# Attention prologue: the first pair's 1/std row on ScalarE's queue, z's projection one step behind its transposes, its exps one group behind, and group norm's power ahead of z's

## The chip, the cores and the metric

The kernel runs on one core of one Trainium2 chip. A core has five engines that run their own instruction streams in order: TensorE (PE, with its weight loads shown apart as PEld), VectorE (DVE), ScalarE (ACT), GpSimd (POOL) and SyncE (SP, which here only starts DMA transfers). The metric is the device time in microseconds (us) of one execution. The kernel before took 3403.12 us (median of three runs, 3402.76 to 3403.5).

## The reference

Two attention layers, each added to its input x of 128 rows x 256 positions x 256 channels, in float32. The change touches only what comes ahead of layer 0.

```python
# layer 0
x = x + attention0(_gn(x), z)              # group norm over 32 groups, no weights
# in attention0, m = _gn(x):
m_norm = layer_norm(m, ln_m_w, ln_m_b)     # per position: needs 1/std of each position
z_norm = layer_norm(z, ln_z_w, ln_z_b)     # z: 256 x 256 x 128
q, k, v = (m_norm @ W.T for W in (Wq, Wk, Wv))   # 8 heads of 32
b = (z_norm @ Wb.T).transpose(...)         # one bias per head, query and key
p = softmax(q @ k.T * scale + b)
o = (p @ v) * sigmoid(m @ Wg.T + bg)
# layer 1
x = x + banded_attention(_gn(x))           # 4 heads of 64, band of 16
```

So before layer 0 can begin, two things are wanted of all of x and all of z: the mean and 1/std of each group of channels of x, and exp(b), a table of 8 x 256 x 256 numbers that every row of the layer multiplies its exponentials by.

## The kernel before

The work has three stages: the prologue, layer 0's loop over 64 pairs of rows, and layer 1's loop over 64 pairs. The order within the prologue and the loops is written out by hand: each engine executes its instructions in the order in which the program emits them, and a tile framework adds the waits.

**z.** The 256 x 256 positions of z come in 16 jobs of 2 MB. `z_front` (L1057) loads a job into one of three buffers `zt`, takes its statistics on DVE (16 `bn_stats`, L1069), and has GpSimd raise the variance to the power -1/2 (`zrs`, L1078). `z_back` (L1081) is called one job later. It works in two steps for each job, four for each group of two jobs: 16 transposes on PE into four PSUM tiles `ps_t` (L1092; three buffers), four copies by ScalarE into `zT` (L1094; ten buffers), and four matmuls on four column tiles of 32 that project onto the 8 heads, into `ps_b` (L1097; eight PE instructions, two passes for each float32 matmul). After the fourth step, ScalarE copies `ps_b` to `bT` (L1104), PE turns it back (`ps_k`, L1107), DVE multiplies by 1/std (`bt`, L1113) and ScalarE takes eight exps into the table `eb` (L1118).

**x.** Between the jobs, eight blocks of x (4 MB each, `x_block`, L1123) are loaded and their group statistics taken on DVE (L1127). After the last, in the body of job 8, `x_moments` (L1129) and `moments_steps` (L961) merge them: a matmul for the mean (L966), one for the variance (L975), a power on GpSimd (`rs_l`, L979), and copies that spread the result over channels (L984).

**The first pair.** The function `starts` (L1404) is a generator that is advanced twice for each job, in the middle of z's statistics and at the end of the body. In turn it runs the moments, loads of pairs 0 to 2 of x, `centre` and `scale` (group norm on GpSimd, L1175 and L1178), `moments` and `root` (1/std of each position, L1188 to L1199), `fetch` (L1204), `turn` (transposes, L1215, then the multiplication by the row on GpSimd, L1221), and the first projections of q and k (L1234, L1238). `root` ends with a DMA that writes the 512 values of 1/std to DRAM (`rs_d`, four-byte pieces, 2 KB); `fetch` reads them back as a row broadcast to all 128 partitions (`rs_r`, 256 KB). Both stand in SyncE's queue, which is also that of all loads of z and x. When job 15 is through, pair 1 is centred, scaled and measured, and layer 0's loop begins with `now.scores(0, 0)` (L1268).

Of the kernel before, what the change touches and what calls it, by code (L numbers as in the profile page):

```python
# [9 lines left out]
F32 = mybir.dt.float32  # L10
AF = mybir.ActivationFunctionType
# [5 lines left out]
P = 128  # L17
# [4 lines left out]
def bcast(ap, axis, n):  # L22

    ap = ap.unsqueeze(axis)
    shape = list(ap.shape)
    shape[axis] = n
    return ap.broadcast_to(shape)
# [746 lines left out]
def fast_kernel(  # L774
# [25 lines left out]
    nc = tc.nc  # L800
    S, I, C = x.shape
    CZ = z.shape[2]
    H = wbT.shape[1]
# [4 lines left out]
    NB = I // P  # L808
    KC = C // P
    NP = S // 2  # L810
    N2 = 2 * I
# [97 lines left out]
    eb = const.tile([P, H, NB, I], F32, name="eb")  # L909
# [9 lines left out]
    for a in range(KC):  # L919
        for h in range(H1):  # L920
            n = P // H1
# [11 lines left out]
    for h in range(H1):  # L933
        n = P // H1
# [9 lines left out]
    bz_r = const.tile([P, H], F32, name="bz_r")  # L944
# [45 lines left out]
    pps = tc.alloc_tile_pool(name="pre_ps", bufs=2, space=PSUM)  # L990

    def mm(name):
        return ps_mm.tile([P, 512], F32, name=name, tag="mm")
# [5 lines left out]
    for w, dst in ((wq, qb), (wk, kb)):  # L999
        for m in range(KC):  # L1000
            ps = mm("b_ps")
            for k in range(KC):
                nc.tensor.matmul(
                    ps[:, 0:1], w[:, k, m * P : (m + 1) * P], lnb_c[:, k : k + 1],
                    start=(k == 0), stop=(k == KC - 1),
# [36 lines left out]
    nga = S // GA  # L1042
# [6 lines left out]
    IB, IS = 32, 64  # L1049
    zjobs = [(b, i) for b in range(NB) for i in range(0, I, IB)]  # L1050
    z_rows = z.rearrange("(u t) (p b) c -> t p u (b c)", t=NB, b=NB)
    wbz = pz.tile([P, 4, 4, H], F32, name="wbz")
# [4 lines left out]
    def z_front(b, i0):  # L1057

        nonlocal zrs
        zt = pz.tile([P, IB, CZ], F32, name="zt", tag="zt", bufs=3)  # L1060
        nc.sync.dma_start(
            zt.rearrange("p (u b) c -> p u (b c)", b=NB), z_rows[b, :, i0 // NB : (i0 + IB) // NB, :]
        )

        st = pz.tile([P, IB, 3], F32, name="zst", tag="zst", bufs=2)
        for i in range(0, IB, 2):
            if i == IB // 2:
                step()
            nc.vector.bn_stats(  # L1069
                st[:, i : i + 2, :].rearrange("p i f -> p (i f)"),  # L1070
                zt[:, i : i + 2, :].rearrange("p i c -> p c i"),
            )
        at = i0 % IS
        if at == 0:
            zrs = pz.tile([P, IS], F32, name="zrs", tag="zrs", bufs=3)
        rs = zrs[:, at : at + IB]
        nc.vector.tensor_scalar(rs, st[:, :, 2], 1.0 / CZ, 1e-5, ALU.mult, ALU.add)
        nc.gpsimd.tensor_tensor(rs, rs, mhalf[:, :IB], ALU.pow)  # L1078
        return zt, zrs

    def z_back(b, i0, zt, rs):  # L1081
        nonlocal ps_b
        at = i0 % IS
        if at == 0:
            ps_b = pps.tile([P, 512], F32, name="ps_b", tag="bias", bufs=1)
        for j in range(at // 16, (at + IB) // 16):
            zTs = []
            for g in range(4):
                ps_t = pps.tile([P, 512], F32, name="ps_t", tag="zT", bufs=3)
                i = (4 * j + g) * 4 - at  # L1090
                for a in range(4):
                    nc.tensor.transpose(ps_t[:, a * P : (a + 1) * P], zt[:, i + a, :], ident)  # L1092
                zT = pz.tile([P, 512], F32, name="zT", tag="zT", bufs=10)
                nc.scalar.copy(zT, ps_t)  # L1094
                zTs.append(zT)
            for g in range(4):
                nc.tensor.matmul(  # L1097
                    ps_b[32 * g : 32 * (g + 1), :], wbz[:, j].rearrange("p a h -> p (a h)"), zTs[g],
                    start=(j == 0), stop=(j == 3),
                )  # L1100
        if at + IB < IS:
            return
        bT = pz.tile([P, 512], F32, name="bT", tag="bT", bufs=2)
        nc.scalar.copy(bT, ps_b)  # L1104
        ps_k = pps.tile([P, 4, 4, 4, H], F32, name="ps_k", tag="keys", bufs=1)
        for a in range(4):
            nc.tensor.transpose(  # L1107
                ps_k[:, a].rearrange("p g j h -> p (g j h)"), bT[:, a * P : (a + 1) * P], ident
            )
        bt = pz.tile([P, IS, H], F32, name="bt", tag="bt", bufs=2)  # L1110
        for j in range(4):
            q = slice(j * 16, (j + 1) * 16)
            nc.vector.tensor_tensor(  # L1113
                bt[:, q, :].rearrange("p (g a) h -> p g a h", g=4), ps_k[:, :, :, j, :].rearrange("p a g h -> p g a h"),
                bcast(rs[:, q].rearrange("p (g a) -> p g a", g=4), 3, H), ALU.mult,
            )
        for h in range(H):
            nc.scalar.activation(  # L1118
                eb[:, h, :, b * P + (i0 - at) // NB : b * P + (i0 - at + IS) // NB],
                bt[:, :, h].rearrange("p (u b) -> p b u", b=NB), AF.Exp, bias=bz_r[:, h : h + 1],  # L1120
            )

    def x_block(j):  # L1123
        xa = px.tile([P, GA * NB, C], F32, name="xa", tag="xa", bufs=2)
# [24 lines left out]
    NT = 2 * NB  # L1149
    x1 = [dram.tile([GB, I, C], F32, name=f"x1_{j}") for j in range(S // GB)]  # L1150
    rs_d = [dram.tile([NT * P], F32, name=f"rs_d{p}") for p in range(NP)]
# [8 lines left out]
    class Pair:  # L1160
# [35 lines left out]
        def root(self):  # L1196

            nc.gpsimd.tensor_tensor(self.rs, self.rs, mhalf[:, :NT], ALU.pow)
            nc.sync.dma_start(rs_d[self.p].rearrange("(t p) -> p t", p=P), self.rs)  # L1199

        def fetch(self):

            self.rs_r = la.tile([P, NT * P], F32, name="rs_r", tag="rs_r", bufs=2)
            nc.sync.dma_start(self.rs_r, rs_d[self.p].unsqueeze(0).broadcast_to([P, NT * P]))  # L1204


        def turn(self, pss=None):
            self.xgT = la.tile([P, KC, N2], F32, name="xgT", tag="xgT", bufs=2)
            self.xnT = la.tile([P, KC, N2], F32, name="xnT", tag="xnT", bufs=2)
            if pss is None:  # L1210
                ps = ps_s.tile([P, KC, N2], F32, name="ps_x", tag="s")
                pss = [ps[:, k, :] for k in range(KC)]
            for k in range(KC):
                for t in range(NT):
                    nc.tensor.transpose(  # L1215
                        pss[k][:, t * P : (t + 1) * P], self.xg[:, t, k * P : (k + 1) * P], ident
                    )
            for k in range(KC):
                nc.scalar.copy(self.xgT[:, k, :], pss[k])
            for k in range(KC):  # L1220
                nc.gpsimd.tensor_tensor(self.xnT[:, k, :], self.xgT[:, k, :], self.rs_r, ALU.mult)  # L1221

# [175 lines left out]
    def pair(p):  # L1398
        return Pair(p) if p < NP else Nobody()

    zrs = ps_b = la = lb = ps_s = ps_o = M0 = R0 = None
    now = nxt = nn = None

    def starts():  # L1404

        nonlocal la, M0, R0, now, nxt, nn
        steps = x_moments()
        next(steps)
        yield
        next(steps)  # L1410
        yield
        next(steps)
        px.release()
        la = tc.alloc_tile_pool(name="l0_early", bufs=1, side="left", reuse_waits="tile")
        now = pair(0)
        yield
        M0, R0 = next(steps)
        now.centre()
        now.scale()
        yield  # L1420
        nxt = pair(1)
        yield
        now.moments(0)
        now.moments(1)
        now.root()
        yield
        nn = pair(2)
        yield
        yield
        now.fetch()  # L1430
        yield
        now.turn([mm("ps_x") for _ in range(KC)])
        yield
        yield
        now.project("qT", 0)
        now.project("kT", 0)
        yield

    start = iter(())

    def step():
        next(start, None)


    behind, nx = None, 0
    with tc.manual_schedule():
        for n, job in enumerate(zjobs):
            front = z_front(*job)
            if behind is not None:
                z_back(*behind)  # L1450
            behind = (*job, *front)
            if nx < nga and nx * 9 <= n * nga:
                x_block(nx)
                nx += 1
                if nx == nga:
                    start = starts()
            step()
        assert nx == nga
        z_back(*behind)
        for _ in start:  # L1460
            pass
        for f in ("centre", "scale"):
            getattr(nxt, f)()
        for r in range(2):
            nxt.moments(r)
# [8 lines left out]
    with tc.manual_schedule():  # L1474
        old = was = Nobody()
        es = nn3 = None
        for p in range(NP):

            nxt.root()
            ps = now.scores(0, 0)  # L1480
            e = now.add_bias(0, 0, ps)
            was.apply(1, 1, es)
# [30 lines left out]
            now.project("gT", 1)  # L1513
            now.gate(0, 1)
            nxt.turn()
            was.normalize(0)
            now.values(1)
            now.keep_values(1)
# [16 lines left out]
            old, was, now, nxt, nn = was, now, nxt, nn, nn3  # L1535
# [39 lines left out]
    with tc.tile_pool(name="l1", bufs=2) as sb, tc.tile_pool(  # L1575
        name="l1s", bufs=4
    ) as sm, tc.tile_pool(name="ps1_mm", bufs=2, space=PSUM) as ps_mm, tc.tile_pool(
        name="ps1_s", bufs=1, space=PSUM
# [160 lines left out]
        def pair1(p):  # L1739
            return Pair1(p) if p < NP else Nobody()  # L1740
# [15 lines left out]
        now, nxt = pair1(0), pair1(1)  # L1756
# [15 lines left out]
        with tc.manual_schedule():  # L1772
            was = Nobody()
            for p in range(NP - 1):
                nn = pair1(p + 2)
# [23 lines left out]
                was, now, nxt = now, nxt, nn  # L1799
# [87 lines left out]
```

## Time and profile before

| | busy us | share of the span |
|---|---|---|
| PE | 3253.1 | 96% |
| PEld | 2041.4 | 60% |
| DVE | 2027.8 | 60% |
| ACT | 1463.2 | 43% |
| POOL | 1974.5 | 58% |

The profile's span is 3403.3 us. Shares over the whole span say little of the prologue, which ends at 269.64 us with the first scores, 8% of the span. These groups of instructions, taken from the stretch 0 to 270 us, are its work:

| line, engine, what | count | busy us | mean ns |
|---|---|---|---|
| L1069 DVE bn_stats of z | 256 | 86.5 | 416 |
| L1127 DVE bn_stats of x | 128 | 77.2 | 684 |
| L1078 POOL power of z's variances | 16 | 86.8 | 5430 |
| L1092 PE transposes of z | 512 | 75.7 | 305 |
| L1097 PE projection of z | 256 | 66.1 | 691 |
| L1094 ACT copies of the transposes | 128 | 66.9 | 594 |
| L1118 ACT exps | 56 | 17.1 | 387 |

A PE time of one instruction includes its pipeline, so overlapping instructions add up to more than the stretch they fill; start-to-start distances are the better measure there.

### The profile page before, as it was taken

To read this page: it belongs to the slowest core of one execution; us is meant where nothing else is said; L and a number is where in the kernel's file an instruction comes from. 1 tells how busy PE (TensorE), PEld (TensorE's weight loads), DVE (VectorE), ACT (ScalarE), POOL (GpSimd) and SP (SyncE) were. 2 spreads that over 40 slices of the span, in tenths; PEclk is the share of its full clock that TensorE was granted. 3 is DMA by queue.
4 is the path that set the end of the run, shared out by engine and by line. 5 is a ranking of instruction groups with operands and counts; after the bars stand their busy time and mean duration, and the time that the engine had idled before them with its cause. 6 is when DMAs were issued, how large, how long until landed. Compare 5 with 4: busy or idle time off the path is not lost. (4 is left out here: it accounts for less than half of the span.)

```text
span 3403.3 us, 81181 instructions
## 1 busy us (share of the span) xinstructions
PE 3253.1 (96%) x35158; PEld 2041.4 (60%) x35158; DVE 2027.8 (60%) x3218; ACT 1463.2 (43%) x2121; POOL 1974.5 (58%) x1377
## 2 busy tenths in 40 slices
PE   5479999999999999999999999799999999999998
PEld 3245555555555555555555555577676777767676
DVE  6955566676666666666666665366544444344455
ACT  2244444444444444444444443344444444444443
POOL 2357778877777777877787775233333333333332
PEclk8789999999999999999999999899999999999999
DMA  9941122222221222222122211212111121211211
GB/s 333 376 133 27 47 73 73 73 48 73 73 73 48 73 73 60 61 73 72 42 69 68 73 48 57 77 52 64 52 57 59 52 64 52 62 54 52 64 57 53
DMA packets 198815, 262.91 MB, mean 77 GB/s; under 512 B 46288, under 2 KB 147536, under 8 KB 197296
## 3 DMA queue, kind: packets, MB, share of 16 engines
q1 hardware_dynamic: 198448, 257.61, 24.9%
q8 instruction: 279, 4.57, 0.7%
q14 instruction: 88, 0.72, 0.1%
HBM read 188.82 MB, written 68.75 MB: 76 GB/s over the span
## 5 line engine op out<-in xcount | busy, mean ns | idle before, releaser
L1289 POOL TENSOR_TENSOR eboth<-e 128x512 f32<-128x512 f32 x512 | 640.5, 1273 | 379.2 <-DVE e L1284 361.7
L1284 DVE TENSOR_TENSOR e<-ps_sc,eb 128x1024 f32<-128x1024 f32 x512 | 603.0, 1219 | 316.1 <-ACT ps_sc L1275 226.5
L1275 ACT ACTIVATE ps_sc<-ps_sc 128x1024 f32<-128x1024 f32 x512 | 492.7, 1006 | 506.6 <-PE ps_sc L1268 506.6
L1676 POOL TENSOR_TENSOR e<-e,bw 128x384 f32<-128x384 f32 x256 | 259.9, 1038 | 443.3 <-ACT e L1674 443.3
L1637 PE MATMUL ps_p<-xgT,w_in 128*128 128x512 f32 x1024 | 468.4, 600 | 0.1
L1629 POOL TENSOR_TENSOR xt<-xt,bout_r 128x1024 f32<-128x1024 f32 x64 | 152.4, 2381 | 382.7 <-PE ps_x L1626 382.7
L1729 DVE TENSOR_TENSOR yo<-ps_y,xt 128x512 f32<-128x512 f32 x128 | 88.4, 690 | 379.6 <-PE ps_y L1725 379.6
L1637 PEld LDWEIGHTS ps_p<-xgT,w_in 128*128 128x128 f32 x1024 | 188.6, 190 | 199.1 <-issue 166.0
L1268 PE MATMUL ps_sc<-qT,kT 32*128 32x256 f32 x4096 | 293.7, 400 | 0.8 <-ACT kT L1238 0.8
L1299 PE MATMUL ps_ov<-e,v 128*32 128x256 f32 x4096 | 274.1, 385 | 0.5 <-DVE oT L1313 0.5
L1234 PE MATMUL ps_p<-xnT,wq 128*128 128x512 f32 x512 | 254.2, 618 | 0.7 <-POOL xnT L1221 0.6
L1234 PE MATMUL ps_p<-xgT,wg 128*128 128x512 f32 x512 | 253.9, 618 | 0.0
L1725 PE MATMUL ps_y<-w_out,oT 128*128 128x256 f32 x1024 | 249.8, 387 | 2.6 <-DVE oT L1710 2.6
L1341 PE MATMUL ps_y<-wo,oT 128*128 128x256 f32 x1024 | 244.8, 382 | 7.1 <-POOL oT L1331 7.1
L1341 PEld LDWEIGHTS ps_y<-wo,oT 128*128 128x128 f32 x1024 | 196.3, 192 | 88.4 <-issue 59.7
L1249 PE MATMUL ps_v<-wv,xnT 128*128 128x256 f32 x1024 | 242.2, 379 | 1.3 <-ACT qT L1238 1.3
L1268 PEld LDWEIGHTS ps_sc<-qT,kT 32*128 32x128 f32 x4096 | 185.4, 184 | 92.5 <-issue 70.7
L1234 PE MATMUL ps_p<-xnT,wk 128*128 128x512 f32 x512 | 240.6, 592 | 0.0
L1652 PE MATMUL ps_v<-w_in,xgT 128*128 128x256 f32 x1024 | 231.8, 379 | 0.0
L1707 DVE RECIPROCAL rv<-odd 128x256 f32<-128x256 f32 x128 | 224.4, 1753 | 4.4
L1652 PEld LDWEIGHTS ps_v<-w_in,xgT 128*128 128x128 f32 x1024 | 194.4, 190 | 53.5 <-issue 30.1
L1249 PEld LDWEIGHTS ps_v<-wv,xnT 128*128 128x128 f32 x1024 | 189.6, 190 | 52.5 <-issue 30.6
(163 smaller groups left out, 5019.8 us busy)
## 6 DMA issues: line engine op xcount, KB each, us to landing
zt<-in_z_dram SPq DMA_DIRECT2D x16, 2048.0 KB
xa<-in_x_dram SPq DMA_DIRECT2D x8, 4096.0 KB
xt<-in_x_dram SPq DMA_DIRECT2D x64, 512.0 KB
rvb<-rsum SPq DMA_DIRECT2D x256, 128.0 KB
x<-xo SPq DMA_DIRECT2D x16, 2048.0 KB
xt<-x SPq DMA_DIRECT2D x64, 512.0 KB
out_dram<-yo SPq DMA_DIRECT2D x63, 512.0 KB
rs_r<-rs_d SPq DMA_DIRECT2D x64, 256.0 KB
```

The source lines that it names most:

```text
L1234: nc.tensor.matmul(ps, w[:, k, m * P : (m + 1) * P], getattr(self, src)[:, k, :], start=(k == 0), stop=(k == KC - 1),)
L1249: nc.tensor.matmul(self.ps_v[:, b * C : (b + 1) * C], self.xnT[:, k, t * P : (t + 1) * P], wv[:, k, :], start=(k == 0), stop=(k == KC - 1),)
L1268: nc.tensor.matmul(self.pss[q // 2][:, q % 2, b, :], self.kT[rs, c, r * I + b * P : r * I + (b + 1) * P], self.qT[rs, c, r * I : (r + 1) * I],
L1275: nc.scalar.activation(self.pss[a], self.pss[a], AF.Exp)
L1284: nc.vector.tensor_tensor(e, pss[a], eb[:, h : h + 2], ALU.mult)
L1289: nc.gpsimd.tensor_tensor(t, es[a][:, :, 0, :], es[a][:, :, 1, :], ALU.add)
L1299: nc.tensor.matmul(ov[q * D0 : (q + 1) * D0, :], self.v[:, r, b, h * D0 : (h + 1) * D0], es[q // 2][:, q % 2, b, :], start=(b == 0), stop= ...
L1341: nc.tensor.matmul(self.ps_y[:, b * C : (b + 1) * C], self.oT[r][:, k, b * P : (b + 1) * P], wo[:, k, :], start=(k == 0), stop=(k == KC - 1),)
L1637: nc.tensor.matmul(ps, w_in[:, k, n * C + m * P : n * C + (m + 1) * P], self.xgT[:, k, :], start=(k == 0), stop=(k == KC - 1),)
L1652: nc.tensor.matmul(ps[:, b * C : (b + 1) * C], self.xgT[:, k, t * P : (t + 1) * P], w_in[:, k, 2 * C : 3 * C], start=(k == 0), stop=(k == ...
L1676: nc.gpsimd.tensor_tensor(e[:, q], e[:, q], bcast(bw.rearrange("p b w -> p (b w)"), 1, KC), ALU.mult)
L1725: nc.tensor.matmul(ps[:, b * C : (b + 1) * C], self.oT[r][:, k, b * P : (b + 1) * P], w_out[:, k, :], start=(k == 0), stop=(k == KC - 1),)
```

## The change

Four edits, all in the prologue.

1. **The 1/std row through ScalarE's queue.** The DMA that was the last line of `root` becomes a method `send`, and both `send` and `fetch` take the queue as an argument. For pair 0 it is ScalarE's: `send` in the statistics of job 13, `fetch` in those of job 15. All other pairs keep SyncE's. SyncE's queue is then left to the loads of z and x.
2. **z's projection one step behind.** `z_back` emits a step's transposes and copies, then the projection of the step before (`z_project`), so that PE needn't stand and wait for the copies of what it has just transposed.
3. **Exps one group behind.** The exps of a group (`z_exp`) are emitted with the third step of the next group, so that ScalarE doesn't stop its copies for `bt`.
4. **Group norm's steps by a plan.** The generator gives way to a table `plan` of (jobs since the last block of x, quarter of a job). The second moments matmul comes after a quarter of job 9's statistics instead of a half, and `rs_l`'s power after three quarters, which puts it ahead of z's power for that job on GpSimd. The transposes of pair 0 move to the end of job 14, the multiplication by the row (`normal`, split off `turn`) to the end of job 15, and the first projections of q and k behind the last exps.

```diff
     def z_back(b, i0, zt, rs):
...
+            z_project()
+            turned = (b, i0 - at, rs, j, zTs)
+
+    def z_project():
+        nonlocal turned, ps_b
+        if turned is None:
+            return
+        (b, i0, rs, j, zTs), turned = turned, None
+        if j == 0:
+            ps_b = pps.tile([P, 512], F32, name="ps_b", tag="bias", bufs=1)
+        for g in range(4):
+            nc.tensor.matmul(
+                ps_b[32 * g : 32 * (g + 1), :], wbz[:, j].rearrange("p a h -> p (a h)"), zTs[g],
+                start=(j == 0), stop=(j == 3),
+            )
+        if j == 1:
+            z_exp()
+        if j < 3:
+            return
         bT = pz.tile([P, 512], F32, name="bT", tag="bT", bufs=2)
...
+        weighed.append((b, i0, bt))
...
-            nc.sync.dma_start(rs_d[self.p].rearrange("(t p) -> p t", p=P), self.rs)
-
-        def fetch(self):
+
+        def send(self, queue=nc.sync):
+            queue.dma_start(rs_d[self.p].rearrange("(t p) -> p t", p=P), self.rs)
+
+        def fetch(self, queue=nc.sync):
...
+    plan = {
+        (0, 4): begin, (1, 1): lambda: next(steps), (1, 3): lambda: next(steps), (1, 4): take, (2, 3): norm,
+        (3, 4): weigh,
+        (5, 3): lambda: now.send(nc.scalar),
+        (6, 4): lambda: now.turn([mm("ps_x") for _ in range(KC)]),
+        (7, 2): lambda: now.fetch(nc.scalar),
+        (7, 4): lambda: now.normal(),
+    }
...
         z_back(*behind)
-        for _ in start:
-            pass
+        z_project()
+        z_exp()
+        now.project("qT", 0)
+        now.project("kT", 0)
```

In the plan, `begin` starts the merge of x's moments, `take` loads pair 0, `norm` spreads the group norm's result, centres and scales pair 0 and loads pair 1, and `weigh` takes pair 0's moments with their power and loads pair 2. In layer 0's loop `nxt.root()` is followed by `nxt.send()` and `nxt.turn()` by `nxt.normal()`, so its order stays as it was.

## The prediction

> **What bounds the kernel now.** I first read the slices of the whole span (85 us each), then cut the opening into stretches that I chose by what the engines were doing.
>
> ```profile
> PEclk8789999999999999999999999899999999999999
> DMA  9941122222221222222122211212111121211211
> ```
> ```profile
> 143.00:165.00 22.00, 0.22 (x3) 0.00 (x0) 21.93 (x49) 2.44 (x8) 6.70 (x2) 0.60 1.03 375
> ...
> 198.00:210.00 12.00, 11.52 (x71) 6.40 (x69) 0.46 (x2) 6.63 (x13) 5.43 (x1) 0.97 0.29 42
> 210.00:219.00 9.00, 1.71 (x13) 1.50 (x14) 0.29 (x1) 0.14 (x1) 0.00 (x0) 0.82 1.07 354
> 219.00:230.00 11.00, 3.54 (x16) 2.93 (x15) 10.66 (x35) 4.83 (x13) 5.61 (x2) 0.50 0.97 309
> ```
>
> The columns are stretch, length, busy us (instructions) of PE, PEld, DVE, ACT, POOL, then granted clock, DMA share, GB/s. Up to 165 us the DMA engines are full (share over 1) and DVE works 21.93 of 22 us: nothing in the diff touches that, so I leave it unchanged. After 165 the transfers stop filling the engines, yet in 210 to 230 PE works 5.25 of 20 us. From the first pair's scores at 269.64 us on, the slices show PE at 9, so time taken out ahead of them comes off the end one for one. The whole question is how long 165 to 270 becomes. Its timeline (start, length, engine, line; idle time and its releaser in brackets):
>
> ```profile
> 171.57 3.35 PEld L1092 LDWEIGHTS ps_t<-ident,zt 128*128 128x128 f32 x16
> ...
> 196.91 0.37 SPq L1199 DMA_DIRECT2D rs_d<-lrs  x1
> ...
> 197.99 0.37 SPq L1061 DMA_DIRECT2D zt<-in_z_dram  x1
> ```
> ```profile
> 203.76 1.93 PE L1097 MATMUL ps_b<-zT,wbz 128*32 128x512 f32 x8
> ...
> 204.64 0.14 PEld L1097 LDWEIGHTS ps_b<-zT,wbz 128*32 128x32 f32 x2 [0.35 <-ACT zT L1094]
> 205.62 1.80 PEld L1092 LDWEIGHTS ps_t<-ident,zt 128*128 128x128 f32 x16 [0.84 <-issue]
> ...
> 207.26 4.51 SPq L1204 DMA_DIRECT2D rs_r<-rs_d  x1
> ...
> 218.71 5.38 DVE L1069 BATCH_NORM_STATS2 zst<-zt 128x6 f32<-128x256 f32 x16 [20.22 <-DMA zt<-in_z_dram]
> ...
> 225.16 2.44 ACT L1118 ACTIVATE eb<-bt,bz_r 128x64 f32<-128x64 f32 x8 [15.01 <-DVE bt L1113]
> ...
> 269.64 1.15 PE L1268 MATMUL ps_sc<-qT,kT 32*128 32x256 f32 x16
> ```
>
> Call 16 transposes T, the projection of their result P. The reader should see three things. The 2 KB write of the 1/std row goes out at 196.91; z's load 1 us behind it on the same queue lands only at 218.71. P waits for ScalarE's copies of the T just made, so one T to the next takes 3.83 us (201.79 to 205.62). And ScalarE's exps wait for DVE behind a whole job of statistics, holding back the next copies.
>
> By differences of T starts, 171.57 to 269.64 (98.1 us) divides into 16 steps of 3.83 (61.3), 1.5 for a cold clock, 5.3, 18.6 and 5.2 extra at the group ends near 190, 210 and 248, 1.3 at the last, 0.9 for the pair's transposes and 3.1 for its projections; about 1 is rounding and small waits. The middle end is 13.4 above its neighbours: the price of the late load.
>
> **What the Trainium skill says.** "DMA: Bandwidth & Descriptors", section "Queues, rings and completion order": SyncE and ScalarE each own a row of rings, but on the same 16 DMA engines, which take turns between rows by packet. The trace has only SyncE's queue, so it shows the blocking within one row (0.37 us of issue, 10.35 us until the read of the row could go), not the relief. "TensorE: Matmul & The Clock Gate", Part 1: after an idle window of about 3.4 us the array runs at half rate. The trace agrees: clock 0.50 in 219 to 230, and T at 171.57 takes 3.35 us instead of 1.80. "TensorEngine Tiling (Array Packing)", "Key Properties": tiles run independently, changing the mode drains. The trace agrees: 16 column-tiled ps_ov matmuls of 256 columns at 278.69 take 1.07 us together, where a full-width pass of 512 columns (L1234) takes 0.43, so 16 in a row would take 3.4.
>
> **Part by part.** I let the new order start where PE is released.
>
> Moments in quarters: 4 bn_stats stand before the second moments matmul instead of 8; 8 take 2.74 us, so PE's T starts 1.37 earlier, at 170.2. Power first: the group norm's power ran 179.62 to 185.05 behind z's and held DVE 7.98 us. Now it can start near 173 and end near 178, before DVE needs it at about 182. The price is z's power 5.4 later, which no bt needs for two jobs. This frees DVE, not PE, directly; I book nothing more for it.
>
> Projection one step behind: P finds its input copied long before. T is 1.80 of weight loads plus 0.17 of switching. P alone is not shown. Lower bound: 8 passes of 0.43 on 4 column tiles, 0.86, plus 0.2 of loads. Upper: if a tile's second pass blocks the other tiles, 5 steps of 0.43, 2.15. The ps_ov row speaks for the lower; I take 1.1, so a step is 3.1 instead of 3.83. ScalarE's four copies, 2.05, fit beneath it. 16 steps: 49.6.
>
> Group ends: P, then ScalarE's bT, then ps_k still stand in line: 0.68 wait and 0.42 transposes, 1.2 with switching, at four places. The exps now stand after the third step of the next group, when their bt has long been made; their 2.44 on ScalarE fill three PSUM buffers and cost PE about 1.2 (copies end 0.6 after T, exps to 4.95, fourth transpose tile at 5.5 instead of 4.3), also four times. Together 9.6, against 3 x 5.2 = 15.7 now besides the late load.
>
> ScalarE's queue: send stands behind job 11's copies, which by my count end near 200.5; its power ends near 200.4 (GpSimd: 178, z 5.4, centring and scaling 4.7, two more powers 10.9, its own 1.0). So no wait for ScalarE; behind it are job 12's copies and then PE. Issue is 0.37 on SyncE; I take the same, and 6.5 (the longest issue of z) as the bad end. Fetch comes two jobs later, 10 us suffice. The late load disappears: -13.4. SyncE then loads z by buffers alone. A load may go when the T of three jobs before is done, and lands some 8.5 later (issued 234.84, moving until 242.3, seen about a microsecond after). My steps give, for jobs 11 to 15:
>
> | job | buffer free, load goes | lands | PE wants it |
> |---|---|---|---|
> | 11 | 178 | 186 | 194 |
> | 12 | 185 | 194 | 201 |
> | 13 | 193 | 201 | 209 |
> | 14 | 200 | 209 | 217 |
> | 15 | 208 | 216 | 225 |
>
> So PE, not the transfers, sets the pace of 7.4 to 8.6 per job; DVE (5.4 of statistics) and GpSimd (5.43 of power) stay under it.
>
> Tail, worse: q and k now come last, behind the last exps; from ps_k to the first scores is 0.58 now (269.06 to 269.64) and will be 5.8. Sum: 170.2 + 1.6 cold + 49.6 + 9.6 + 1.0 (pair's transposes) + 1.8 (last P and wait) puts the last ps_k at 233.8. Then bt 1.7, exps 2.4, two casts of q and k 1.4, 0.3 to the scores: 239.6 instead of 269.64. GpSimd's normal, centring and scaling (2.5 + 4.7) follow the last z power, near 226, and fit. In the first pair the exps no longer sit between scores and q's cast (ps_v came 6.05 after the scores, now about 5): 1 us more. Saved 31: **3403 - 31 = 3372**.
>
> **Rivals.**
> - **A, transfers still collide:** the small write keeps engines slow for about 10 us on either queue, so job 14's or 15's load comes up to 13.4 late against 8.6 of slack at PE; job 15's power on GpSimd, the row's multiplication behind it and q and k behind that then end some 6 later: 3378. For it: the same 16 engines. Against: their share in 198 to 210 is 0.29, most stand idle, so another row's packets find room.
> - **B, P does not overlap its tiles:** 16 x 1.05 = 17 back, 3389. Against it the ps_ov row.
> - **C, tighter steps:** P hidden to 0.8 (4.8) and exps absorbed by the PSUM buffers (3 of 4.8): 3364. For it: PE fetches weights ahead (six loads in 0.20 us at 254.28).
> - **D, slower:** B's 17, and two ScalarE issues that each hold it 6.5 and wait out 10.4 for the write: 3372 + 17 + 13 + 10 = 3412. For it: SyncE shows such issues.[...]
>
> **How the numbers follow.** Forecast 0.54, A 0.15, B 0.08, C 0.19, D 0.04. The range must take in A and C with their spread, and drops D and part of B: 3360 to 3384. Slower by over 0.2% (above 3410) only in D, 0.03; within 0.2% 0.03, from D's lighter forms; faster 0.94.
>
> **What would show it.** Right: first scores (L1268) near 240; DVE's 20 us wait for z gone; one T to the next near 3.1; waits of ps_b's weight loads for ScalarE near zero; R's copy without its 8 us wait; clock near 1 from 175 on. Wrong: ScalarE idle on the send; ps_t waiting for z's DMA after 190; P still near 1.9; first scores before 230 or after 255; or another period of the later loops, which I hold at today's.

## The result, and the profile after

The changed kernel took **3376.15 us** (median of four runs, 3374.71 to 3377.0) against 3403.31 us for the kernel before in the same series: a ratio of 0.992, with a 95% interval of 0.9903 to 0.9937. The forecast was 3372, so the saving came out at 27 us instead of 31.

The spans of the two profiles differ by 28.8 us (3403.3 and 3374.5). The first pair's scores start 26.3 us earlier (269.64 and 243.35). From there to the end of layer 0's loop 2.2 us are saved, 1.5 of them in the first pair, whose second scores follow after 6.43 us instead of 7.97. The passage between the layers gives 1.0 more, and layer 1 takes 0.7 back. So the case is decided ahead of the first scores.

First the page of the changed kernel, the clock and the DMA share in 40 slices of 84 us:

```profile
PEclk8699999999999999999999999899999999999999
DMA  9951212221222222122212221121111211212111
```

The loops look as before. What changed is visible only in the opening, cut into stretches (columns: stretch, length, busy us of PE, PEld, DVE, ACT, POOL with instruction counts, granted clock, DMA share, GB/s), again of the changed kernel:

```profile
143.00:165.00 22.00, 2.70 (x12) 0.63 (x11) 21.37 (x45) 1.21 (x3) 6.84 (x2) 0.50 1.03 376
198.00:210.00 12.00, 10.13 (x83) 6.62 (x82) 9.49 (x31) 8.62 (x20) 9.12 (x4) 1.00 1.00 210
210.00:219.00 9.00, 7.85 (x67) 5.20 (x65) 2.85 (x9) 8.13 (x21) 4.02 (x1) 1.00 0.95 218
219.00:230.00 11.00, 8.96 (x73) 5.61 (x72) 9.15 (x30) 5.51 (x11) 6.14 (x2) 1.00 0.28 92
230.00:240.00 10.00, 6.22 (x28) 2.40 (x29) 0.90 (x5) 5.34 (x14) 9.92 (x5) 0.83 0.01 2
```

Up to 165 us almost nothing moved. In 210 to 230 PE now works 16.81 of 20 us at full clock, where before it worked 5.25 of 20 us at a clock of 0.82 and then 0.50. Two things are not as they should be. In 198 to 210 the DMA engines are fully busy (share 1.00) but move only 210 GB/s. And in 210 to 219 DVE is idle for two thirds of the time, though it still has two jobs of z to measure. The timeline of the changed kernel (start, length, engine, line; idle time and its releaser in brackets) shows both and what came of them:

```profile
180.07 1.81 PEld L1091 LDWEIGHTS ps_t<-ident,zt 128*128 128x128 f32 x16 [0.84 <-ACT zT L1093]
182.05 0.16 PEld L1106 LDWEIGHTS ps_b<-zT,wbz 128*32 128x32 f32 x8 [0.17 <-issue]
182.05 1.07 PE L1106 MATMUL ps_b<-zT,wbz 128*32 128x512 f32 x8
183.04 1.29 PEld L1091 LDWEIGHTS ps_t<-ident,zt 128*128 128x128 f32 x12 [0.84 <-ACT zT L1093]
...
200.82 7.52 SPq L1061 DMA_DIRECT2D zt<-in_z_dram  x2
200.96 0.40 ACTq L1218 DMA_DIRECT2D rs_d<-lrs  x1
...
216.15 5.42 DVE L1069 BATCH_NORM_STATS2 zst<-zt 128x6 f32<-128x256 f32 x16 [6.82 <-DMA zt<-in_z_dram]
...
223.57 5.42 DVE L1069 BATCH_NORM_STATS2 zst<-zt 128x6 f32<-128x256 f32 x16 [1.78 <-DMA zt<-in_z_dram]
...
229.13 0.88 DVE L1124 TENSOR_TENSOR bt<-ps_k,zrs 128x128 f32<-128x128 f32 x4
230.05 2.43 ACT L1135 ACTIVATE eb<-bt,bz_r 128x64 f32<-128x64 f32 x8 [3.08 <-DVE bt L1124]
233.00 0.66 PE L1091 MATMUL ps_t<-ident,zt 128*128 128x128 f32 x4 [4.34 <-ACT zT L1093]
...
243.35 1.15 PE L1289 MATMUL ps_sc<-qT,kT 32*128 32x256 f32 x16 [1.28 <-ACT kT L1259]
```

Read the top four lines first. The projection (128*32, eight passes) takes 1.07 us and no longer waits for ScalarE; one T to the next is 183.04 - 180.07 = 2.97 us. In the list of waits from 165 to 260 us the projection's weight loads waited 8.2 us for ScalarE before; that entry is gone. Then follow the middle: z's load for job 14 goes out at 200.82, the row's write at 200.96 on the other queue, without ScalarE having to wait for it. DVE then waits 6.82 us for that load (job 14's statistics, 216.15). Its statistics of job 15 come late too (223.57), and the multiplication of group 6's `bt` (229.13) stands behind them in DVE's order. ScalarE waits 3.08 us for `bt`, PE waits 4.34 us for ScalarE's copies behind the exps, and its clock sinks to 0.83. The late load is smaller than before, but it is still there.

### The profile page after: what moved, and what is told of

The parts are those of the page before. It is cut to its first block, busy times and chain, and to the rows that moved or that the text cites. A ratio compares the mean times of both kernels' runs of the same rounds, so it can differ in the third digit from the quotient of the medians.

```text
span 3374.5 us, 81186 instructions
## 1 busy us (share of the span) xinstructions
PE 3228.6 (96%) x35158; PEld 2036.5 (60%) x35158; DVE 2025.4 (60%) x3218; ACT 1463.9 (43%) x2121; POOL 1975.0 (59%) x1377
```

## The experiments

The expectations set two accounts of the late load against each other. **H1**: the 2 KB write still holds job 14's load, although it sits in another queue. **H2**: z comes late because of its buffers or its bandwidth, and `bt` stands behind job 15's statistics anyway. A third possibility for the 4 us that were missing at the first scores is that a step of the sum was booked too low. Beyond that, each of the four edits was undone or made alone. All times are medians; the ratio is to the kernel before in the same series, which stayed between 3403.3 and 3404.0. "First T" is where PE starts the first 16 transposes after x's moments.

| run | us | ratio, 95% interval | first T at | first scores at |
|---|---|---|---|---|
| kernel before | 3403.31 | | 171.57 | 269.64 |
| the change | 3376.15 | 0.9903 to 0.9937 | 170.41 | 243.35 |
| e1_row16 | 3372.17 | 0.9891 to 0.9921 | 171.57 | 239.67 |
| e2_rowpe | 3370.90 | 0.9887 to 0.9918 | 170.47 | 238.99 |
| e3_sync | 3377.33 | 0.9909 to 0.9937 | 171.24 | 244.86 |
| e8_double | 3377.05 | 0.9910 to 0.9937 | 170.73 | 243.32 |
| e4_samestep | 3379.30 | 0.9914 to 0.9941 | 170.37 | 245.89 |
| e5_expsnow | 3389.51 | 0.9943 to 0.9971 | 170.11 | 254.86 |
| e6_powerafter | 3378.64 | 0.9912 to 0.9940 | 171.30 | 245.58 |
| e7_queuealone | 3396.23 | 0.9967 to 0.9985 | 172.24 | 261.13 |
| e10_adjacent | 3378.62 | 0.9912 to 0.9939 | 170.40 | 246.87 |
| e11_apart | 3372.03 | 0.9894 to 0.9924 | 170.33 | 237.88 |
| e12_samestep_row | 3378.76 | 0.9912 to 0.9939 | 170.08 | 245.74 |
| e9_best | 3365.00 | 0.9873 to 0.9903 | 171.58 (job 9's) | 232.07 |

Among e1, e2, e3, e8, e10 and e11, whose edits all come behind first T, it still varies between 170.33 and 171.57. So where two runs differ by little more than a microsecond at the first scores, the distance from first T to the scores is the better measure; it is 72.94 us in the changed kernel.

### Does the write hold the load? The row in fewer pieces

e1 writes the row of pair 0 in 128 pieces of 16 bytes, and the multiplication reads it in that order.

```diff
-            queue.dma_start(rs_d[self.p].rearrange("(t p) -> p t", p=P), self.rs)
+            how = "(p t) -> p t" if self.p == 0 else "(t p) -> p t"
+            queue.dma_start(rs_d[self.p].rearrange(how, p=P), self.rs)
...
-                nc.gpsimd.tensor_tensor(self.xnT[:, k, :], self.xgT[:, k, :], self.rs_r, ALU.mult)
+                        self.rs_r.rearrange("p (q t) -> p t q", t=NT), ALU.mult,
```

> The changed kernel, with pair 0's 1/std row written as 128 pieces of 16 bytes instead of 512 of 4 (same 2 KB, same queue, same moment); the row is read back in that order and the multiplication on GpSimd reads it with a stride. H1 (the pieces of the write take turns with z's packets on the same DMA engines and hold job 14's load back): a quarter of the pieces holds it a quarter as long, about 2 us instead of 8; DVE's 6.8 us wait for job 14's z shrinks to about 1, ScalarE's 3.1 us wait for bt and PE's 4.3 us wait go, first scores near 239 instead of 243.35, 3371 to 3372. H2 (z comes late because of buffers or bandwidth, and bt sits behind job 15's statistics anyway): nothing moves, 3376.

e2 turns the row on PE first, so that four pieces of 512 bytes remain.

```diff
+                ps = mm("ps_rs")
+                nc.tensor.transpose(ps[:NT, :P], self.rs, ident)
+                rsT = la.tile([NT, P], F32, name="rsT", tag="rsT", bufs=1)
+                nc.scalar.copy(rsT, ps[:NT, :P])
+                queue.dma_start(rs_d[self.p].rearrange("(t p) -> t p", p=P), rsT)
```

> The changed kernel, with pair 0's 1/std turned on PE to 4 rows of 128 (one transpose, one ScalarE copy more), so that the write is 4 pieces of 512 bytes. H1 (number of pieces): no hold at all, z's load of job 14 lands 8.5 us after its issue, as others do; first scores near 239, 3371, no later than the 16-byte version. H2 (buffers or bandwidth): 3376. A third reading, that any write on ScalarE's queue holds SyncE's loads whatever its pieces: 3376 as well, but with z's rate low after the send.

They took 3372.17 and 3370.9 us, close to H1's figures. The same places of the timeline, now of e2 (line numbers below the send are up to 7 higher):

```profile
202.51 0.51 ACTq L1223 DMA_DIRECT2D rs_d<-rsT  x1
...
217.09 5.42 DVE L1069 BATCH_NORM_STATS2 zst<-zt 128x6 f32<-128x256 f32 x16 [1.73 <-DMA zt<-in_z_dram]
...
222.66 0.89 DVE L1124 TENSOR_TENSOR bt<-ps_k,zrs 128x128 f32<-128x128 f32 x4
...
227.34 2.46 ACT L1135 ACTIVATE eb<-bt,bz_r 128x64 f32<-128x64 f32 x8
...
233.62 0.66 PE L1118 MATMUL ps_k<-ident,bT 128*128 128x128 f32 x4 [0.78 <-ACT bT L1115]
...
238.99 1.15 PE L1296 MATMUL ps_sc<-qT,kT 32*128 32x256 f32 x16 [1.27 <-ACT kT L1266]
```

Careful with the second line: here it is job 15's statistics that start at 217.09; job 14's began at 209.73 without a wait, where the changed kernel had 216.15. `bt` of group 6 is made ahead of job 15's statistics, and the exps wait for nothing. The last `ps_k` is at 233.62 and the scores at 238.99. H1 holds in its main point, that this write delays that load, and H2 falls: with the hold gone, the sum of the prediction (233.8 and 239.6) fits to 0.6 us, so no large term was missing from it. The fit is in part luck. Sixteen steps of 2.97 us are 2.1 less than the 49.6 booked, while the first step, with PE's clock still low, cost about 2.5 more than another (170.41 to 177.05 in the changed kernel) where 1.6 was booked.

### Which property of the write? Twice as many pieces, and neighbours against pieces apart

e8 sends the changed kernel's write a second time, to a tensor that nobody reads.

```diff
             queue.dma_start(rs_d[self.p].rearrange("(t p) -> p t", p=P), self.rs)
+            if self.p == 0:
+                queue.dma_start(rs_d2.rearrange("(t p) -> p t", p=P), self.rs)
```

> The changed kernel, with the 512 four-byte pieces of pair 0's row written a second time, into a DRAM tile that nothing reads, right behind the first on ScalarE's queue. H1: engines held some 8 us longer, so the loads of jobs 14 and 15 land later by about that; PE's stop at the last exps grows from 4.3 to about 12, 3383 to 3385. H2: two more issues on ScalarE, 0.4 us each, 3376 to 3377.

The expectation of 3383 to 3385 was missed: 3377.05 us, and DVE waits the same 6.82 us, though the packets of ScalarE's queue rose from 672 to 1200. The hold does not grow with the number of pieces. So the next pair kept the number and changed only where the pieces lie. Both are e2 with an extra write of 512 four-byte pieces, read by nobody, ahead of the row's own; in e10 they are neighbours in DRAM, in e11 512 bytes apart.

```diff
+    rs_x = dram.tile([NT * P], F32, name="rs_x")            # e10
+                queue.dma_start(rs_x.rearrange("(t p) -> p t", p=P), self.rs)
...
+    rs_x = dram.tile([NT * P, 128], F32, name="rs_x")       # e11
+                queue.dma_start(rs_x[:, 0].rearrange("(t p) -> p t", p=P), self.rs)
```

> The version with pair 0's row in 4 pieces of 512 bytes (3370.9), with an extra write that nothing reads, at the place and on the queue of the send: the same 512 values of 1/std in pieces of 4 bytes, next to each other in DRAM as in the changed kernel. If the write itself holds job 14's load, whatever waits for it: z's rate falls for some 8 us again and 3375 to 3377. If it was the order of send and fetch: 3371.

> As the run before, with the 512 four-byte pieces of the extra write 512 bytes apart in DRAM instead of next to each other. If the number of pieces holds the engines: 3375 to 3377, as with neighbours. If it is that neighbours share memory words and wait for each other: z's rate stays up, 3371 to 3372.

e10 took 3378.62 us (3376.51 to 3379.8; its median is 1.6 above the 3375 to 3377 expected), e11 3372.03 (3370.66 to 3373.72), with 680 packets in that queue in both. From first T the scores come 76.47 us later in e10 and 67.55 in e11. The rate at which z comes in is the direct evidence: stretches of 2 us, with the same columns as above, DMA share and GB/s last. First the changed kernel:

```profile
204.00:206.00 2.00, 1.29 (x13) 0.54 (x6) 2.00 (x7) 1.10 (x3) 2.00 (x1) 1.00 1.19 311
206.00:208.00 2.00, 2.00 (x22) 1.74 (x23) 2.00 (x7) 1.36 (x3) 0.63 (x1) 1.00 1.13 55
208.00:210.00 2.00, 2.00 (x18) 1.16 (x15) 1.29 (x6) 1.08 (x3) 1.40 (x1) 1.00 1.17 85
210.00:212.00 2.00, 2.00 (x18) 0.90 (x16) 0.00 (x0) 2.00 (x6) 2.00 (x1) 1.00 1.02 63
```

e10, neighbours:

```profile
208.00:210.00 2.00, 2.00 (x18) 0.99 (x17) 1.46 (x7) 1.40 (x3) 1.23 (x1) 1.00 0.99 47
210.00:212.00 2.00, 2.00 (x23) 1.44 (x20) 0.00 (x0) 1.74 (x4) 2.00 (x1) 1.00 0.51 36
212.00:214.00 2.00, 2.00 (x20) 1.29 (x12) 0.00 (x0) 2.00 (x8) 2.00 (x1) 1.00 0.87 60
214.00:216.00 2.00, 0.86 (x9) 0.58 (x12) 0.00 (x0) 2.00 (x7) 0.20 (x1) 1.00 0.40 39
216.00:218.00 2.00, 2.00 (x20) 1.26 (x13) 0.93 (x3) 1.13 (x4) 0.00 (x0) 1.00 0.50 88
```

e11, pieces apart:

```profile
206.00:208.00 2.00, 2.00 (x21) 1.26 (x19) 1.97 (x9) 1.91 (x4) 0.61 (x1) 1.00 0.57 172
208.00:210.00 2.00, 2.00 (x19) 1.65 (x16) 1.92 (x7) 1.14 (x4) 2.00 (x1) 1.00 0.69 201
210.00:212.00 2.00, 2.00 (x18) 0.99 (x17) 2.00 (x7) 2.00 (x7) 2.00 (x1) 1.00 1.07 380
```

And one stretch of e2, which has no small pieces at all:

```profile
208.00:210.00 2.00, 2.00 (x18) 0.99 (x17) 1.97 (x9) 1.25 (x3) 0.91 (x1) 1.00 0.33 68
```

With neighbours z falls to 55 to 85 GB/s for 6 us in the changed kernel and to 36 to 88 for 10 us in e10. e11's dip to 172 is no such hold: it lies between two loads, like the lower one of e2 (68, with a share of 0.33). In e11 the next load goes out at 207.42 and job 14's statistics start at 208.20 without a wait. So what costs is that very small pieces are written side by side, and the reader of the row is not to blame, since nobody reads the extra write.

The pieces themselves do not fill the engines' time. By the packet records of the changed kernel's trace, 525 packets of ScalarE's queue pass in 203 to 206.5 and take 9.6% of the 16 engines' time. In 207 to 214, when z is slow, there are 2 of them, while z's 635 packets take 92.8% of the time and move 0.65 MB. e10 shows the same order: 2 packets of ScalarE's queue in 211 to 218, and 404 of z that move 0.41 MB. So the write's own packets are through before z slows, and it is z's packets that then take long. H1's wording in e1's expectation, that the pieces take turns with z's packets, is not what happens, and e11 sends as many packets through the same queue and engines at no cost.

The Trainium skill, "DMA: Bandwidth & Descriptors", section "Specifications", says that below 512 bytes the DMA does a read-modify-write. That would let neighbouring pieces wait for one another where pieces apart need not, and e2's pieces of 512 bytes fit it. But e1's neighbouring pieces of 16 bytes did no such harm (371 GB/s in 206 to 208), and e8's second write added none. No run here shows the read-modify-write itself, and why z's packets go on being slow after the write's own are through stays open.

### What is the other queue worth?

e3 keeps everything but has both transfers in SyncE's queue.

```diff
-        (5, 3): lambda: now.send(nc.scalar),
+        (5, 3): lambda: now.send(),
...
-        (7, 2): lambda: now.fetch(nc.scalar),
+        (7, 2): lambda: now.fetch(),
```

> The changed kernel, with pair 0's send and fetch back on SyncE's queue, at the same places of the plan. H1: job 14's load now stands behind the whole write (10 us) instead of sharing engines with it; it lands 2 to 3 us later than in the changed kernel (near 219 instead of 216), 3378 to 3380: the queue itself is worth little, the moment of the write more. If the queue is what removed the late load (the reason that the prediction gave, 13.4 us booked): 3385 to 3389.

e7 does the reverse: the kernel before, with only pair 0's two transfers moved to ScalarE's queue.

```diff
-            nc.sync.dma_start(rs_d[self.p].rearrange("(t p) -> p t", p=P), self.rs)
+            queue = nc.scalar if self.p == 0 else nc.sync
+            queue.dma_start(rs_d[self.p].rearrange("(t p) -> p t", p=P), self.rs)
```

> The kernel before, with nothing changed but pair 0's two transfers of the 1/std row, which go on ScalarE's queue at the places where they stood. H1 (the write holds z's load on either queue): job 12's load comes 3 to 5 us earlier than in the kernel before, no more; ScalarE waits some 3 us for the power ahead of job 10's copies: 3397 to 3403. If the queue is what removes the late load, as the prediction booked: job 12 lands near 207 and 13 us go: 3388 to 3391.

The timeline of e3:

```profile
201.14 0.37 SPq L1218 DMA_DIRECT2D rs_d<-lrs  x1
201.69 10.46 SPq L1061 DMA_DIRECT2D zt<-in_z_dram  x2
...
218.66 5.41 DVE L1069 BATCH_NORM_STATS2 zst<-zt 128x6 f32<-128x256 f32 x16 [8.39 <-DMA zt<-in_z_dram]
```

And of e7:

```profile
185.47 2.04 PE L1092 MATMUL ps_t<-ident,zt 128*128 128x128 f32 x16
...
187.55 0.37 SPq L1061 DMA_DIRECT2D zt<-in_z_dram  x1
...
197.59 0.40 ACTq L1200 DMA_DIRECT2D rs_d<-lrs  x1
...
198.73 1.12 PE L1092 MATMUL ps_t<-ident,zt 128*128 128x128 f32 x4 [6.71 <-ACT zT L1094]
...
199.08 5.41 DVE L1069 BATCH_NORM_STATS2 zst<-zt 128x6 f32<-128x256 f32 x16
...
217.54 5.39 DVE L1069 BATCH_NORM_STATS2 zst<-zt 128x6 f32<-128x256 f32 x16 [0.75 <-DMA zt<-in_z_dram]
```

The kernel before, at the same transposes and the power that its send waits for:

```profile
184.52 2.04 PE L1092 MATMUL ps_t<-ident,zt 128*128 128x128 f32 x16
...
195.87 1.01 POOL L1198 TENSOR_TENSOR lrs<-lrs,mhalf 128x4 f32<-128x4 f32 x1
```

In the changed kernel the queue is worth 1.2 us in the medians, which their ranges do not separate, and 0.7 us from first T to the scores; e3's 3377.33 lies just below the 3378 to 3380 expected. In the order of before the queue is worth 7.6 us. The reason is z's load at 187.55 in e7: it goes as soon as the T that frees its buffer has ended (185.47 and 2.04 us). In the kernel before that T ended at 186.56 (184.52 and 2.04 us), yet the load could only go at 197.99. There the send stood ahead of it in SyncE's queue, waiting for GpSimd's power until 196.9, and the load waited over 10 us behind a wait that was not its own, before the write cost it anything. In e7 ScalarE takes that wait over, and PE stands 6.71 us for its copies; part of the gain goes there. In the changed kernel the plan issues the send only when its power is ready (GpSimd ends it at 200.3), so that no queue waits.

e7's 3396.23 lies just below the 3397 to 3403 expected, and its account of job 12 was wrong. That job's load came through before the write went out, and its statistics start at 199.08 without a wait, against 218.71 before. The write then slowed the next load, job 13's: it goes out at 204.96, z comes at 28 and 99 GB/s in 206 to 210, and its statistics start at 217.54.

So **the late send and the other queue remove the same wait**, and given the late send the queue adds little. What the late send is worth alone is read from these waits; no run keeps the early send in the changed kernel.

The Trainium skill, "DMA: Bandwidth & Descriptors", section "Issuing engines are not separate DMA queues", has it that starting transfers from several engines saves only the issuing time. Here the issue is 0.37 us and the gain 7.6: in e7 what is saved is the wait at the head of the queue.

### Projection in the same step, exps at once, power behind

e4 lets each step project its own transposes again, in the changed kernel; e12 does the same on e2.

```diff
-            z_project()
             turned = (b, i0 - at, rs, j, zTs)
+            z_project()
```

> The changed kernel, with the projection of a step again right behind the step's own copies; everything else as changed. My account: a step goes back from the 2.97 us that the changed kernel shows to 3.83, 16 times, 13.8; the stop at the last exps (4.3) shrinks since a slower PE wants z later: 3385 to 3390. Rival (the gain came from the late load and the exps; PE would have waited for ScalarE or DVE anyway): 3376 to 3379.

> The version with pair 0's row in 4 pieces of 512 bytes (3370.9), with the projection again in the same step as its transposes. My account of the small 3 us that this edit cost in the changed kernel: there it also took bt out from behind job 15's late statistics, which gave back 4 to 5. Without the late load nothing is given back: first scores 7 later than 238.99, 3377 to 3379. Rival (the projection's place is worth 3 us by itself): 3374.

In both a step is 3.83 us again. e12 lost 6.75 us at the first scores and 7.9 in the median against e2 (7.1 from first T to the scores). e4 lost only 3 us against the changed kernel: 3379.30 misses the 3385 to 3390 expected and lies at its rival's 3376 to 3379. Its timeline shows why:

```profile
224.41 0.88 DVE L1124 TENSOR_TENSOR bt<-ps_k,zrs 128x128 f32<-128x128 f32 x4
```

Projected at once, group 6 ends within its own job, so its `bt` stands ahead of job 15's statistics in DVE's order and does not suffer from the late load (224.41, where the changed kernel has 229.13). e12, without the hold, speaks against that rival, which had 3374 there: 3378.76. The edit and the hold interact, and undoing one edit in the presence of the other under-rates it.

e5 emits the exps as soon as `bt` is emitted.

```diff
         weighed.append((b, i0, bt))
+        z_exp()
```

> The changed kernel, with a group's eight exps emitted right behind its bt, as in the kernel before. My account: ScalarE waits there for DVE, which reaches bt only behind the next job's statistics: waits of bt near 3, 5 and 9 us at the group ends near 191, 205 and 221, against 1.2 each for the exps in their new place: 3383 to 3389. Rival (PSUM's three buffers and the zT buffers absorb it): 3375 to 3378.

It took 3389.51 us, 13.4 more than the change and just beyond what was expected. From its timeline:

```profile
215.81 2.43 ACT L1136 ACTIVATE eb<-bt,bz_r 128x64 f32<-128x64 f32 x8 [3.33 <-DVE bt L1124]
...
218.76 1.11 PE L1091 MATMUL ps_t<-ident,zt 128*128 128x128 f32 x4 [4.26 <-ACT zT L1093]
```

This is the pattern of every group end: ScalarE waits 1.8 to 3.3 us for `bt`, PE waits 2.7 to 4.3 for ScalarE, buffers of z come free later, and DVE then waits for z (6.15 and 6.28 us). DVE's third wait, 7.37 us for job 14, has another cause: that load goes out beside the write (207.89 and 208.03), so it is held as in the changed kernel. Undone alone in the changed kernel, this edit costs most; the late send was not undone alone, and part of this edit's cost may be the hold's.

e6 puts the group norm's power behind z's again.

```diff
-        (1, 3): lambda: next(steps), (1, 4): take,
+        (1, 4): lambda: (next(steps), take()),
```

> The changed kernel, with group norm's power again behind job 9's power of z (the step of the plan at three quarters of job 9 moved to its end). My account, nothing booked for PE: DVE waits some 3 us for R, GpSimd's chain ends 1.5 later, the send may hold ScalarE 1 us: 3376 to 3378. Rival (the 8 us wait of DVE that the earlier power removed was on the path): 3381 to 3384.

```profile
186.13 2.44 DVE L984 COPY R_l<-rs_l 128x256 f32<-128x256 f32 x1 [2.42 <-POOL rs_l L979]
```

3378.64 us, 2.5 more and 0.6 above the 3376 to 3378 expected; from first T to the scores it is 1.3. Most of that comes through the hold: the send goes 1.3 later, counted from first T, PE waits 0.67 us for z where the changed kernel has no wait, and 4.86 instead of 4.34 behind the last exps. What the edit is worth without the hold, no run shows.

This line of e6 shows DVE waiting 2.42 us for the power and then copying for 2.44 us beside GpSimd's centring, which takes 2.36. In the changed kernel the same copy takes 0.30, though it too runs beside GpSimd, in the middle of z's power:

```profile
178.33 5.43 POOL L1078 TENSOR_TENSOR zrs<-zrs,mhalf 128x32 f32<-128x32 f32 x1
...
182.45 0.30 DVE L984 COPY R_l<-rs_l 128x256 f32<-128x256 f32 x1
```

The Trainium skill, "SBUF — State Buffer", section "Who interferes with whom", says that some DVE copies share a port with GpSimd, and that the later of the two stands still until the first has ended. Beside the centring the trace agrees (2.44 against 0.30 us); beside the power it does not, and the measurement decides: not every GpSimd instruction holds this copy.

### A version that beats both

e9 is e2 with the transposes of job 8 put ahead of the moments' matmuls, in the time in which PE waits for the statistics of x, and with the send a little later.

```diff
                 if nx == nga:
                     ended = n
+                    z_back(*behind)
+                    behind = None
...
-        (5, 3): lambda: now.send(nc.scalar),
+        (6, 1): lambda: now.send(nc.scalar),
```

> The version with pair 0's row in 4 pieces of 512 bytes (3370.9), with two more moves: job 8's transposes and projections emitted ahead of the moments matmuls, so that PE does them while it waits for x's statistics (24 us idle up to 168 in the changed kernel), and the send a job later, since GpSimd's power for it would now come after ScalarE. My account: one job of 7.2 us leaves the stretch from 170 on, first scores near 232, 3364. If GpSimd's powers (8 x 5.43 and 8 more from 173 on, the last near 222) or z's loads set the pace instead: 3367 to 3371.

```profile
151.15 1.99 PE L1091 MATMUL ps_t<-ident,zt 128*128 128x128 f32 x16
...
209.59 5.42 DVE L1069 BATCH_NORM_STATS2 zst<-zt 128x6 f32<-128x256 f32 x16 [0.17 <-DMA zt<-in_z_dram]
...
232.07 1.15 PE L1296 MATMUL ps_sc<-qT,kT 32*128 32x256 f32 x16 [1.28 <-ACT kT L1266]
```

3365.0 us, where 3364 was expected: 11 less than the change and 38.7 less than the kernel before in its series. Job 8 is done at about 154 us, when PE had nothing else, DVE hardly waits for z (0.17 us), and the scores start 6.9 us ahead of e2's.

## Why the prediction was right, and where it was wrong

**The frame held.** Time taken out ahead of the first scores came off the end nearly one for one: 26.3 us there, 28.8 in the span. The first pair gave 1.5 us instead of the 1 booked.

**The steps held.** T starts at 170.41 (170.2 forecast). The group norm's power runs from 172.94 to 178.37 (173 to 178). P alone is 1.07 us, with 1.1 taken from bounds of 1.06 and 2.15, so the four column tiles do work side by side and rival B is out. A step is 2.97 instead of 3.1; a step at a group's end is 187.32 to 191.45, 1.16 above that (1.2 booked); one with exps, 183.04 to 187.32, is 1.31 above it (1.2 booked).

**The send held.** Its power ended at 200.3 (200.4) and it went out at 200.96 (200.5) for 0.40 us, with no wait of ScalarE. Rival D's long issues did not come.

**The step that failed** is "The late load disappears: -13.4", with the reason given against rival A, that most engines stand idle and another row's packets find room. Job 14's statistics were due at 209 and began at 216.15; job 15's load was to land at 216, and its statistics began at 223.57. Rival A had the effect right: the write slows z's load for some 6 to 10 us from another queue as well, and its 3378 lay 2 us above the measurement, the forecast 4 below. Its reason, the same 16 engines, is not enough: e11 sends as many packets through the same engines and holds nothing, and in the changed kernel the write's packets are through when z slows. What the load met were the after-effects of small pieces written side by side. The delay reached PE by another way than A had it: not through GpSimd's power and q and k, but through DVE's order, in which group 6's `bt` stands behind the statistics that wait for the load. That order was in reach of the prediction, which listed what stands behind ScalarE's send but not what stands behind DVE's statistics. At the first scores the whole sum was 3.75 us too early (239.6 against 243.35); the hold alone cost 4.4 there, by e2's 238.99.

**Right for a reason that was only half seen** is the rest of that term. The prediction read the 10 us between the send and the row's read as the time of the write. The trace of before held a second wait of about the same size in front of it, z's load standing behind a send that waited for its power; e7 shows it. And the prediction credited the other queue with what the plan's later send seems to do nearly alone, since putting both transfers back on SyncE's queue costs only 1.2 us (e3). Its remark that after 165 us the transfers stop filling the engines holds for 198 to 210, but not for its own rows of 210 to 230, with shares of 1.07 and 0.97.

**One price was set at nothing and was not nothing.** "Power first" was booked as freeing only DVE; e6 puts it at 1.3 us from first T to the scores and 2.5 in the medians, in the presence of the hold.

**The projection's share was not 16 times the difference of a step.** From 3.83 to 2.97 that would be 13.8 us; e12 against e2 shows 7.1 from first T. With the old order the exps cost 0.44 us a time instead of 1.31, group 3's end falls ahead of the first T, no last P is left over at the end, and the cold start costs 1.1 less; together 6.8. The sum of the prediction had the exps, the ends and the last P on its debit side, which is why the total still came out.

## What to carry to other kernels

A queue is fed by an engine that issues in order: before you weigh a transfer in it, look at what the issuing instruction waits for and which loads stand behind it; issuing it when its data is ready did nearly as much here as another queue. A transfer of a few bytes, in four-byte pieces side by side, can still hold a large one for longer than its own packets take; write it in few, long pieces (here a transpose on PE and a copy, 0.27 and 0.26 us, bought 5 us). And when a load may come late, follow the order of the engine that waits for it: what stands behind the waiting instruction is late too, whoever owns it.

## What the runs showed of the hardware that was not expected

- 512 four-byte pieces written side by side in DRAM hold another queue's 2 MB load at 55 to 85 GB/s for 6 us (the change) or 36 to 88 for 10 us (e10); the same pieces 512 bytes apart, with the same 680 packets, do not (e11). Twice as many neighbours held it no longer (e8).
- The hold begins when the pieces themselves are through: 2 packets of their queue in 207 to 214 us of the changed kernel, against 525 in 203 to 206.5.
- A DMA share above 1 does not mean that much is moved: it was 1.17 at 85 GB/s in the changed kernel, and 1.10 at 371 GB/s in e2. It counts the time that packets take, and in the hold few packets took long.
